# Moving the third image's first-channel products, the norm factors and the last filter chunk of a fused convolution and attention kernel

## The chip, the cores and the metric

The kernel runs on one core of a Trainium2 chip. The metric is the device time of one execution in microseconds (us). Before the change it was 2292.45 us, the median of three runs (2290.4, 2292.45, 2292.69). The engines are named as in the profile: PE is TensorE (PEld its weight loads), DVE is VectorE, ACT is ScalarE, POOL is GpSimd, SP is SyncE, which here only issues DMAs.

## The reference

Eight images of 512 channels by 32x32 pixels in fp32. `_gn` is a group norm over 32 groups, `bn_eval` a scale and shift per channel, and `cbs` a convolution, `bn_eval` and silu.

```python
def bot_attention(x, qkv_w, rw, rh):          # 4 heads of 64, 1024 pixels
    q, k, v = conv2d(x, qkv_w, 0)             # split into heads
    logits = jnp.einsum('bhdi,bhdj->bhij', q, k + (rw + rh)) * HD ** (-0.5)
    a = jax.nn.softmax(logits, axis=-1)
    return jnp.einsum('bhij,bhdj->bhdi', a, v)

t = cbs(_gn(x), cv1_w, cv1_bn, 0)             # 1x1, 512 -> 512
ys = [t[:, :256], t[:, 256:]]
for i in range(2):
    z = cbs(ys[-1], m_cv1_w[i], m_cv1_bn[i], 1)    # 3x3, 256 -> 256
    z = bot_attention(z, m_qkv_w[i], m_rw[i], m_rh[i])
    z = silu(bn_eval(conv2d(z, m_cv2_w[i], 0)))    # 1x1, 256 -> 256
    ys.append(ys[-1] + z)
out = x + cbs(concatenate(ys), cv2_w, cv2_bn, 0)   # 1x1, 1024 -> 512
```

## The kernel before, in words

**Tiling.** An image is held as 128-channel chunks of 1024 pixels. The images go in four pairs (`p` from 0 to 3, `ia` and `ib`); the change concerns the first pair and what precedes it. Line numbers are those of the kernel before, which the profile uses. Work of a later image is done ahead of its pair, where an engine has room: the first 1x1 convolution (`cv1`) of the third image's first 256 output channels (`y0`, two chunks `oc` 0 and 1) is made during the first pair's 3x3 convolution; the rest of it in the attentions.

**Group norm** (`group_norm_part`, L737 on). PE sums the channel means over groups (`gm_ps`), DVE turns them into `gm` and `dev`, PE sums `dev` (`gv_ps`), DVE adds eps (`gr`, L714), POOL takes the power (L715), DVE makes `shift` (L751), and ACT applies scale and shift in place (L757), by chunk `c` and half (512 pixels). Then PE makes the 1x1 products (L503, in `conv1x1`). It is a generator: each `next(norm)` issues one stage.

**The 3x3 convolution** (`conv3x3`) is a Winograd convolution of both images of a pair at once: the input `y1` is transformed by DVE (`tiles_in`, L525 to L580, into `v_in`), the filters by DVE and ACT (`make_u`, below), PE multiplies (L626, `c_ps`), ACT copies a part (`c_m`, L631), and DVE transforms back (L647 to L675) into `z`, which ACT passes through silu (L476). It runs in six turns: two output chunks `oc` by three rows `i` of the transform. In a turn PE makes the products `inner` (`cps` 1 and 2) and then `outer` (0). `between` is a dictionary of callbacks, called before the part `(turn, first cp)`: turn 1 to 6, first cp 1 for the inner and 0 for the outer part.

**Filters** (`make_u`, L390 to L430). A filter chunk is 128 input by 128 output channels of a 3x3 filter. It is transformed in eight steps of a generator: for rows `i` 2, 0, 1 a triple of `tensor_tensor` and a triple of `scalar_tensor_tensor` (L416 to L421, with the ACT copies L414 and L415), and a "mid" triple for row 0 (L398 to L400) and for row 1 (L402 to L404). POOL stores the result to DRAM (L427), and SP loads it later as a unit of the ring buffer `u`. The second convolution's filters (n=1) are made in the first pair: chunk (0,0) by `early` in the first qkv projection, (0,1) and (1,0) in the first attention, (1,1) after it, around `m2_a`.

**Attention** (`attention_fast`). Groups g of 0 to 3 (chunk by half) of eight key blocks, in four pairs of blocks per group. For each pair PE makes logits (L996, `l_ps`), ACT the exponentials (L1000, `pt`), DVE adds them into `acc` (L1014, L1016), PE multiplies by v (L1030, `av_ps`). At the end of a group ACT and DVE empty `av_ps` into z (L1037, L1038), PE sums `acc` over partitions (L1047, `s_ps`), DVE makes the reciprocal `rc`, which goes over DRAM (SP) and comes back spread out as `rs` for the scaling of z (L1102). `av_ps` has one PSUM buffer (`ps_av`); the logits share three (`ps_big`). `behind` is a dictionary of hooks: the key g, or (g, at) with at 1 to 3, is called after that pair of blocks. `hooks` builds it; a step of the filter generator (`step_u`) or of a norm (`step_norm`), or a single extra, may hang on each.

**What sets the order.** Each engine takes its instructions in the order that a scheduler writes down when the kernel is built. It follows the program's order and its own priorities; `tc.issue_after(ins)` adds an edge, so that what is issued inside the block comes after `ins`, if it runs on the same engine. PE orders its products of the third image after a product of the convolution in this way. DMAs stand in the queue of the engine that issues them: SP's for most loads, POOL's for stores and `late` loads.

**Around the change, in order of time:** the second image's norm (about 40 to 46 us) and products, the input transforms of both images, the third image's norm, the convolution (from 77.64) with the third image's products before its turn 3, the first qkv projection, the first attention (`l_ps` from 159.67), `m2_a` and the second projection (224.65 to 267.30), and the second attention (267.30 to about 330).

Of the kernel before, what the change touches and what calls it, by code (L numbers as in the profile page):

```python
# [61 lines left out]
def kernel(  # L62
# [134 lines left out]
    def load_m2(n):  # L197
        nc.sync.dma_start(m2_sb[:, n], m_cv2_w[n].rearrange("(k p) o -> p k o", p=P))

    def make_r(n, raw=None):  # L200
        if raw is not None:
            with tc.issue_after(s.last_exp[0].ins):
                turn_r(n, raw)
            yield
        for c in range(NM):
            for half in range(NH):
                r = act.tile([P, ROWS, F], F32, tag="t", name="r_new", bufs=4)
                tt(
                    r, rw_sb[:, n, c].unsqueeze(1).to_broadcast([P, ROWS, F]),
                    rh_sb[:, n, c, ts(half, ROWS)].unsqueeze(2).to_broadcast([P, ROWS, F]), ALU.add,  # L210
                )
                nc.gpsimd.dma_start(r_dram[n][c][:, ts(half, HALF)], r.rearrange("p h w -> p (h w)"))
                yield
# [258 lines left out]
    def stages(act, small, ps_big, ps_av, n_pt):  # L472
# [7 lines left out]

        shifted, powered, k_added = [None], [None], []
        silu_in, last_product, silued, last_exp, m2_silu = [], [None], [None], [None], [None]

# [10 lines left out]

        def conv1x1(w_of, rhs_of, nk, ks=None, ps=None, ends=None, by_half=False):

# [86 lines left out]
        def conv3x3(n, vs, u_of, z, groups=G, summed=None, after=None, between={}):  # L583
# [10 lines left out]
            for oc in range(NM):  # L594
                dst = z[:, oc].rearrange("p g x -> p (g x)").rearrange("p (t r w) -> p r t w", r=4, w=F)
                for i in range(NI):
# [15 lines left out]
                    for cps in ((1, 2), (0,)):  # L612
                        if (turn, cps[0]) in between:
                            between[turn, cps[0]](product)
                        for row in range(2):
                            for cp in cps:
                                for c in range(2):
                                    ps, bank, at = places[CPS[cp][c]]
                                    to = slots(ps, bank)[:, row, at]
                                    for k in range(NM):  # L620
# [3 lines left out]
                                        for h in range(2):  # L624
                                            o = slice(h * HD, (h + 1) * HD)
                                            product = nc.tensor.matmul(  # L626
                                                to[o], us[cp][:, k, row, c, o], rhs,
                                                start=(k == 0), stop=(k == NM - 1),
                                            )
# [108 lines left out]
        def group_norm_part(xts, by_act=0, behind=lambda c: None, spill=False):  # L738
# [12 lines left out]
            stt(shift, gm, -1.0, gr, ALU.mult, ALU.mult)  # L751
            for c in range(n):
                ahead = behind(c)
                for half in range(NH):
                    part = xts[c][:, ts(half, HALF)]
                    with tc.issue_after(ahead.ins) if ahead else nullcontext():
                        applied = nc.scalar.activation(  # L757
                            part, part, AF.Identity, scale=gr[:, c : c + 1], bias=shift[:, c : c + 1]
                        )
            yield multiplied, read, applied, powered[0]  # L760
# [446 lines left out]

        def cv1_products(w_of, xts, oc, ks=range(NX), ps=None, by_half=False):
            return conv1x1(
                lambda k: w_of(k, oc), lambda k, half: xts[k][:, ts(half, HALF)], NX, ks, ps, (0, NX - 1), by_half  # L1210
            )
# [489 lines left out]
    for p in range(NP):  # L1701
# [68 lines left out]
        if p == 0:  # L1770
            with tc.issue_after(powered.ins):
                first_taps, second_taps = [load_late(0, k, inside(Y2[k])) for k in range(NM)]
        z = new_z()
        t = s.conv3x3(
            0, vs, u_of(0), z, summed=None if direct else z[:, :, 0], after=last_out,
            between={(2, 1): third_norm, (2, 0): third_y0} if direct else {},
        )
        xs = norm = None
        if more:
            if direct:  # L1780
                xs = xs_third
            else:
                xs = [load_x(act, ia + 2, c, NX) for c in range(NX)]
# [36 lines left out]

        def hooks(norms, us=(), extra={}):
            calls = {}
            for g in range(NG):
                for at in range(4):
                    key = (g, at) if at else g
                    calls[key] = [step_norm] if key in norms else []
                    if 4 * g + at in us:
                        calls[key].append(step_u)
                    if key in extra:
# [6 lines left out]
        if p == 0:  # L1836
# [7 lines left out]
            extra[2, 2] = lambda: late_taps.append(load_late(1, 1, inside(Y2[1])))  # L1844
            extra[3, 2] = lambda: make_sq(1, q_tiles, [t[:, j] for t in q_sums for j in range(2)])
        behind = hooks(() if p == 0 else NORM_A, range(16), extra) | {NG: begin_cv1(0, Y1[0], ia + 2)}
        if p == 0:
            behind[NG + 1] = lambda: nxt.go_on()
        end = s.attention_fast(qkv, z[:, :, 0], at_of(ia, 0), behind, at_once=p == 0)
        for made in more_u:  # L1850
            pass
# [36 lines left out]
        else:  # L1888
# [52 lines left out]
        def parts_of(ocs):  # L1941
# [5 lines left out]

        behind = hooks(NORM_B, (), {}) | {
            NG + 1: begin_cv1(1, Y1[1], ia + 3)
# [254 lines left out]
```

## Time and profile before

| What | us |
|---|---|
| median of three runs | 2292.45 |
| the profiled execution, its own time | 2295.04 |
| its span, first to last instruction | 2293.5 |
| PE busy | 2223.7 |
| DVE busy | 1753.5 |
| ACT busy | 1098.3 |
| POOL busy | 205.3 |

The mean granted clock of PE is 0.991 of full speed. PE is busy in 97% of the span. A line of a timeline gives start, length, engine, line, operation, output and inputs, tile shapes, type and count, and in square brackets the idle time before it with what ended it. A line of waits gives the engine, the tile and line that waited, what it waited for, the total, the number of times, and the longest. One logical 128x512 fp32 product counts as two matmul records in the trace. A line of busy time by stage gives the stretch and its length, then for each engine the busy time and the number of instructions, then the granted clock (1.00 is full), the share of the DMA engines and GB/s.

### The profile page before, as it was taken

The numbers are of one execution on the slowest core, as the hardware profiler recorded it, in microseconds if no ns is written. First come the engines' busy times: TensorE is split into PE (matmuls) and PEld (weight loads), VectorE is DVE, ScalarE is ACT, GpSimd is POOL, SyncE is SP. The second block draws the span as 40 slices with busy tenths as digits, with TensorE's granted clock in tenths as the row PEclk, the third lists the DMA queues.
The fourth block names the chain that finished last, engine by engine and source line by source line (L and its number), as shares of the span: only waits on it lengthen the run. The fifth ranks groups of instructions, "written<-read, shape, count | busy, mean of one in ns | idle before, by whom it ended". The sixth has DMA issues, their size and how long they took to land.

```text
span 2293.5 us, 40534 instructions
## 1 busy us (share of the span) xinstructions
PE 2223.7 (97%) x16338; PEld 1083.1 (47%) x16338; DVE 1753.5 (76%) x2701; ACT 1098.3 (48%) x1361; POOL 205.3 (9%) x409
## 2 busy tenths in 40 slices
PE   7899999999999999999999999999999999999997
PEld 3563437443465443734347443654345643473443
DVE  7879789778758689886857868986784868886742
ACT  7445452555225666366323666445622455335533
POOL 2212110000120000000021000000012000000002
PEclk9999999999999999999999999999999999999999
DMA  7743626322473233612168141532137611251115
GB/s 244 276 153 117 216 76 248 106 69 71 107 224 136 75 121 96 213 46 84 52 151 266 33 164 45 169 124 75 57 79 179 215 53 42 70 196 42 48 29 134
DMA packets 128420, 281.06 MB, mean 123 GB/s; under 512 B 34112, under 2 KB 56364, under 8 KB 127200
## 3 DMA queue, kind: packets, MB, share of 16 engines
q1 hardware_dynamic: 100240, 192.25, 26.2%
q0 software_dynamic: 27984, 86.13, 12.6%
q8 instruction: 131, 2.15, 0.4%
q14 instruction: 65, 0.53, 0.1%
HBM read 210.29 MB, written 68.03 MB: 121 GB/s over the span
## 4 chain that ended last, share of the span: by engine, by line
PE 73%; DVE 20%; ACT 3%; issue 2%; DMA 1%; POOL 0%; DVEq 0%; SPq 0%; ACTq 0%; POOLq 0%
PE av_ps L1030 16%; PE l_ps L996 16%; PE c L1248 8%; PE p_ps L886 6%; PE c_new L1248 6%; PE ps L503 6%; PE m_ps L1228 4%; DVE acc L1016 2%; PE pv_ps L892 2%; PE x_ps L1348 2%; PE c_ps L626 2%; DVE c_e L650 1%; PE s_ps L1047 1%; DVE c_t L647 1%; DVE c_t L648 1%
## 5 line engine op out<-in xcount | busy, mean ns | idle before, releaser
L1000 ACT ACTIVATE pt<-l_ps 128x1024 f32<-128x1024 f32 x512 | 495.8, 1023 | 361.3 <-PE l_ps L996 329.5
L1016 DVE TENSOR_TENSOR acc<-acc,pt 128x1024 f32<-128x1024 f32 x384 | 469.9, 1224 | 97.9 <-ACT pt L1000 74.8
L1030 PE MATMUL av_ps<-pt,vT 64*64 64x512 f32 x4096 | 490.4, 596 | 12.6 <-DVE z L1038 12.3
L996 PE MATMUL l_ps<-q,kr 64*64 64x512 f32 x4096 | 488.1, 592 | 1.6 <-ACT pt L1000 0.8
L1030 PEld LDWEIGHTS av_ps<-pt,vT 64*64 64x64 f32 x4096 | 155.6, 133 | 288.3 <-issue 239.8
L996 PEld LDWEIGHTS l_ps<-q,kr 64*64 64x64 f32 x4096 | 158.9, 134 | 274.2 <-issue 253.8
L626 PEld LDWEIGHTS c_ps<-v_in,u 128*64 128x64 f32 x4320 | 235.7, 137 | 5.3 <-issue 5.3
L626 PE MATMUL c_ps<-v_in,u 128*64 128x128 f32 x4320 | 237.5, 273 | 0.0
L1228 PE MATMUL m_ps<-z,m_sb 128*128 128x512 f32 x256 | 112.5, 592 | 0.0
L886 PE MATMUL p_ps<-t_z,sq 128*128 128x512 f32 x224 | 108.0, 601 | 3.6 <-DVE c_t L648 3.6
L631 ACT COPY c_m<-c_ps 128x512 f32<-128x512 f32 x48 | 28.1, 586 | 164.7 <-PE c_ps L626 117.5
L1014 DVE TENSOR_TENSOR acc<-pt 128x1024 f32<-128x1024 f32 x64 | 78.0, 1219 | 36.2 <-ACT pt L1000 36.2
L476 ACT ACTIVATE t<-m_ps,bh,sh 128x512 f32<-128x512 f32 x64 | 46.4, 774 | 86.4 <-PE m_ps L1228 86.4
L886 PE MATMUL p_ps<-z,sq 128*128 128x512 f32 x168 | 80.8, 604 | 0.2 <-ACT m_z L923 0.2
L1298 POOL DMA_DIRECT2D c_out<-in_x_dram x56 | 50.0, 976 | 309.1 <-ACT c_out L476 306.7
L1228 PEld LDWEIGHTS m_ps<-z,m_sb 128*128 128x128 f32 x256 | 48.3, 190 | 58.8 <-issue 56.9
L476 ACT ACTIVATE z<-z,bh,sh 128x512 f32<-128x512 f32 x64 | 47.8, 806 | 27.8 <-DVE z L675 27.8
L476 ACT ACTIVATE c_out<-cz,bh,sh 128x512 f32<-128x512 f32 x14 | 16.7, 1297 | 91.4 <-DVE cz L1325 91.4
L1038 DVE TENSOR_TENSOR z<-av_ps,z 128x512 f32<-128x512 f32 x64 | 44.1, 688 | 20.6 <-ACT z L1037 20.6
L1102 DVE TENSOR_TENSOR z<-z,rs 128x512 f32<-128x512 f32 x64 | 43.9, 687 | 18.8 <-DMA rs<-r_dram 18.4
L886 PEld LDWEIGHTS p_ps<-t_z,sq 128*128 128x128 f32 x224 | 39.2, 192 | 36.1 <-issue 36.1
L647 DVE TENSOR_TENSOR c_t<-c_ps,c_m 128x512 f32<-128x512 f32 (+1 forms) x56 | 34.1, 610 | 28.7 <-ACT c_m L631 28.7
(308 smaller groups left out, 3192.5 us busy)
## 6 DMA issues: line engine op xcount, KB each, us to landing
u<-u SPq DMA_DIRECT2D x135, 512.0 KB
sq<-sq SPq DMA_DIRECT2D x42, 384.0 KB
rs<-r_dram SPq DMA_DIRECT2D x118, 128.0 KB
x<-in_x_dram SPq DMA_DIRECT2D x28, 512.0 KB
r_in<-r SPq DMA_DIRECT2D x28, 512.0 KB
y_in<-y SPq DMA_DIRECT2D x28, 512.0 KB
c_out<-in_x_dram POOLq DMA_DIRECT2D x56, 256.0 KB, 5.4
out_dram<-c_out POOLq DMA_DIRECT2D x56, 256.0 KB, 3.7
```

The lines of the kernel that those rows point to most:

```text
L476: silued[0] = nc.scalar.activation(dst, src, AF.Silu, scale=sh[:, k : k + 1], bias=bh[:, k : k + 1])
L503: last_product[0] = nc.tensor.matmul(ps[:, half, :], w_of(k), rhs_of(k, half), start=(k == begin), stop=(k == end))
L626: product = nc.tensor.matmul(to[o], us[cp][:, k, row, c, o], rhs, start=(k == 0), stop=(k == NM - 1),)
L647: tt(m[:, :, 0::2], slots(inner_ps, 0)[..., qs], m24[..., qs], ALU.add)
L886: nc.tensor.matmul(ps[:, o, :], w[:, o, :], rhs, start=not onto, stop=True, skip_group_check=onto)
L996: nc.tensor.matmul(ps[kh * HD : (kh + 1) * HD, hd, :], kr[r, c, o : o + HD], q[r, c, ts(half, HALF)], start=True, stop=True,)
L1000: last_exp[0] = exp = nc.scalar.activation(pt, ps, AF.Exp, scale=SCALE)
L1014: return nc.vector.tensor_tensor(accs[g], pt[0], pt[1], ALU.add)
L1016: ins = nc.vector.tensor_tensor(accs[g], accs[g], pt[i], ALU.add)
L1030: nc.tensor.matmul(avs[g][hd * HD : (hd + 1) * HD, kh, :], vT[r, j, o : o + HD], pt[i][r, hd, :], start=(j == 0), stop=(j == NJ - 1),)
L1228: nc.tensor.matmul(pss[half][:, oc, :], m2_sb[:, n, k, ts(oc, P)], ao[:, k, ts(half, HALF)], start=(k == 0), stop=(k == NM - 1),)
L1248: nc.tensor.matmul(ps[:, o, :], w[:, k, ts(o, P)], rhs[part][:, c], start=(k == 0 and not onto), stop=(k == KB - 1), skip_group_check=onto,)
```

## The change

Five things change.

1. **Factors ahead of filter steps** (second image's norm). `behind_u` issues three filter steps between the norm's activations; they now come after the norm's addition of eps (`added_eps`, L714) on DVE.
2. **The third image's `y0` products at three places.** Its norm ends in turn 1 (key (1,0)) instead of turn 2, and the third row of the input transforms becomes a step of its own, at (2,1). Chunk 0 (both halves) is made at (2,0), the first half of chunk 1 at (3,1), and its second half after the convolution, ahead of the qkv projection. `conv1x1` and `cv1_products` take `halves`. The silu of a chunk (the eviction of its PSUM tile) comes after its last half. With `spill` the norm's activations are sorted, all first halves ahead of all second halves.
3. **The norm factor ahead of the eviction.** Since the third norm stands at (1,0), its `gr` stands on DVE ahead of the eviction of turn 1's products (L647 on). `conv_product` holds the convolution's latest product.
4. **The DMAs of `make_sq`** are issued on POOL after those of r (`put_r`).
5. **The last filter chunk** (1,1) moves from around `m2_a` into the second attention, one step on each of the hooks 0, 1, 4, 6, 7, 8, 11 and 12 (4g + at). In the first attention the steps hang on hooks 0 to 11 only, and what is left is issued after it. Of the units of the second convolution three are loaded ahead instead of six.

```diff
 def make_r(n, raw=None):
...
-                nc.gpsimd.dma_start(r_dram[n][c][:, ts(half, HALF)], r.rearrange("p h w -> p (h w)"))
+                put_r[0] = nc.gpsimd.dma_start(r_dram[n][c][:, ts(half, HALF)], r.rearrange("p h w -> p (h w)"))
...
 def conv1x1(...):
-            order = [(k, half) for k in ks for half in range(NH)]
+            order = [(k, half) for k in ks for half in halves]
...
 def conv3x3(...):
                         if (turn, cps[0]) in between:
-                            between[turn, cps[0]](product)
+                            between[turn, cps[0]](conv_product[0])
...
 def gn_rstd(...):
-            read = nc.vector.tensor_scalar(gr, ps, GN_EPS, None, ALU.add)
+            added_eps[0] = read = nc.vector.tensor_scalar(gr, ps, GN_EPS, None, ALU.add)
...
 def group_norm_part(...):
-            for c in range(n):
-                ahead = behind(c)
-                for half in range(NH):
-                    part = xts[c][:, ts(half, HALF)]
-                    with tc.issue_after(ahead.ins) if ahead else nullcontext():
-                        applied = nc.scalar.activation(
-                            part, part, AF.Identity, scale=gr[:, c : c + 1], bias=shift[:, c : c + 1]
-                        )
+            parts = [(c, half) for c in range(n) for half in range(NH)]
+            for c, half in sorted(parts, key=lambda a: a[1]) if spill else parts:
+                ahead = behind(c) if half == 0 else ahead
+                part = xts[c][:, ts(half, HALF)]
+                with tc.issue_after(ahead.ins) if ahead else nullcontext():
+                    applied = nc.scalar.activation(
+                        part, part, AF.Identity, scale=gr[:, c : c + 1], bias=shift[:, c : c + 1]
+                    )
...
     def behind_u(c):
         if c == 2:
-            for _ in range(3):
-                next(chunk)
+            with tc.issue_after(s.added_eps[0].ins):
+                for _ in range(3):
+                    next(chunk)
         return copied_u[0] if c else None
...
-    def third_y0(done):
-        y0s = new_y0()
-        for oc in Y0S:
-            ps = ps_av.tile([P, NH, HALF], F32, tag="av", name="ps")
+    third_y0s, third_ps = [], {}
+
+    def third_y0(oc, halves=range(NH)):
+        def run(done):
+            if not third_y0s:
+                third_y0s.extend(new_y0())
+            if oc not in third_ps:
+                third_ps[oc] = ps_av.tile([P, NH, HALF], F32, tag="av", name="ps")
             with tc.issue_after(done.ins):
-                s.cv1_products(w1_of, xs_third, oc, ps=ps, by_half=True)
-            s.cv1(w1_of, xs_third, y0s, None, [oc], {oc: (ps, NX)})
-        keep_y0(G, y0s)
+                s.cv1_products(w1_of, xs_third, oc, ps=third_ps[oc], by_half=True, halves=halves)
+            if NH - 1 in halves:
+                s.cv1(w1_of, xs_third, third_y0s, None, [oc], {oc: (third_ps[oc], NX)})
+
+        return run
...
     def third_norm(done):
         with tc.issue_after(last.ins), tc.issue_after(s.silued[0].ins), tc.issue_after(done.ins):
             next(norm)
+
+    def third_parts(done):
         for g in range(G):
             s.tiles_in(Y1[g], putter(vs, g), [2], ecs[g])
...
+        in_first = {
+            (1, 0): third_norm, (2, 1): third_parts, (2, 0): third_y0(0), (3, 1): third_y0(1, [0]),
+        }
...
-            between={(2, 1): third_norm, (2, 0): third_y0} if direct else {},
+            between=in_first if direct else {},
...
             if direct:
                 xs = xs_third
+                third_y0(1, [1])(s.conv_product[0])
+                keep_y0(G, third_y0s)
...
-            extra[3, 2] = lambda: make_sq(1, q_tiles, [t[:, j] for t in q_sums for j in range(2)])
-        behind = hooks(() if p == 0 else NORM_A, range(16), extra) | {NG: begin_cv1(0, Y1[0], ia + 2)}
+            def with_sq():
+                with tc.issue_after(put_r[0].ins):
+                    make_sq(1, q_tiles, [t[:, j] for t in q_sums for j in range(2)])
+
+            extra[3, 2] = with_sq
+        behind = hooks(() if p == 0 else NORM_A, {i: 1 for i in range(12)}, extra) | {NG: begin_cv1(0, Y1[0], ia + 2)}
...
-        for made in more_u:
+        while step_u():
             pass
...
             if direct:
-                more_u = filters([(1, 1, late_taps[0])])
-                with tc.issue_after(end.scaled.ins):
-                    for _ in range(5):
-                        made = step_u()
-                last = m2_a()
+                m2_a()
                 end.check()
...
-                with tc.issue_after(made.ins), tc.issue_after(last.ins):
-                    for made in more_u:
-                        pass
-                feed(units(1)[:6])
+                feed(units(1)[:3])
...
-        behind = hooks(NORM_B, (), {}) | {
+        if direct:
+            more_u = filters([(1, 1, late_taps[0])])
+        behind = hooks(NORM_B, {i: 1 for i in (0, 1, 4, 6, 7, 8, 11, 12)}) | {
             NG + 1: begin_cv1(1, Y1[1], ia + 3)
         }
...
         end = s.attention_fast(qkv, z[:, :, 1], at_of(ib, 0), behind, at_once=True)
+        while step_u():
+            pass
```

More of the change, by code (lines that the diff above doesn't have):

```diff
@@ L198, in load_m2 @@
         nc.sync.dma_start(m2_sb[:, n], m_cv2_w[n].rearrange("(k p) o -> p k o", p=P))
+    put_r = [None]
     def make_r(n, raw=None):
@@ L479, in silu @@
             return silued[0]
-        shifted, powered, k_added = [None], [None], []
-        silu_in, last_product, silued, last_exp, m2_silu = [], [None], [None], [None], [None]
+        shifted, powered, added_eps, k_added = [None], [None], [None], []
+        silu_in, last_product, silued, last_exp, m2_silu, conv_product = [], [None], [None], [None], [None], [None]
         def exp_table():
@@ L493, in big, with conv1x1 @@
             return ps_big.tile([P, 2, HALF], F32, tag="big", name="p_ps")
-        def conv1x1(w_of, rhs_of, nk, ks=None, ps=None, ends=None, by_half=False):
+        def conv1x1(w_of, rhs_of, nk, ks=None, ps=None, ends=None, by_half=False, halves=range(NH)):
             if ps is None:
@@ L625, in conv3x3 @@
                                             o = slice(h * HD, (h + 1) * HD)
-                                            product = nc.tensor.matmul(
+                                            conv_product[0] = nc.tensor.matmul(
                                                 to[o], us[cp][:, k, row, c, o], rhs,
@@ L1206, in attention_general, with cv1_products @@
             return ao
-        def cv1_products(w_of, xts, oc, ks=range(NX), ps=None, by_half=False):
+        def cv1_products(w_of, xts, oc, ks=range(NX), ps=None, by_half=False, halves=range(NH)):
             return conv1x1(
-                lambda k: w_of(k, oc), lambda k, half: xts[k][:, ts(half, HALF)], NX, ks, ps, (0, NX - 1), by_half
+                lambda k: w_of(k, oc), lambda k, half: xts[k][:, ts(half, HALF)], NX, ks, ps, (0, NX - 1), by_half,
+                halves,
             )
@@ L1819, in begin_cv1, with hooks @@
             return run
-        def hooks(norms, us=(), extra={}):
+        def hooks(norms, us={}, extra={}):
             calls = {}
@@ L1826, in hooks @@
                     calls[key] = [step_norm] if key in norms else []
[L1827 to L1828 removed]
+                    calls[key] += [step_u] * us.get(4 * g + at, 0)
                     if key in extra:
```

## The prediction

> **What bounds the kernel now.** I read the page first (busy time by engine), then TensorE's waits from 30 to 335 us (the stretch that the diff touches), its timeline, VectorE's waits and timeline in that stretch, and busy time by stage. All times are of the profiled execution.
>
> The page puts TensorE at 97% of the span, so only its stalls, and stretches at a lower clock, can be won.
>
> ```profile
> PE 2223.7 (97%) x16338; PEld 1083.1 (47%) x16338; DVE 1753.5 (76%) x2701; ACT 1098.3 (48%) x1361; POOL 205.3 (9%) x409
> ```
>
> TensorE's waits, 30 to 335 us (total, times, longest):
>
> ```profile
> PE av_ps L1030 <- DVE z L1038: 5.6, 4, 3.1
> PE ps L503 <- DVE c_t L648: 4.1, 1, 4.1
> PE c_ps L626 <- DVE v_in L579: 3.3, 1, 3.3
> PE ps L503 <- ACT x_second L757: 2.6, 1, 2.6
> PE ps L503 <- ACT y_half L476: 2.4, 1, 2.4
> PE s_ps L1047 <- DVE acc L1016: 1.5, 1, 1.5
> ```
>
> Some 20 us. Where they lie is in its timeline (start, length, count, idle before):
>
> ```profile
> 46.43 0.70 PE L503 MATMUL ps<-x_second,w_cols 128*128 128x512 f32 x1 [2.58 <-ACT x_second L757]
> ...
> 77.64 7.13 PE L626 MATMUL c_ps<-v_in,u_new 128*64 128x128 f32 x96 [3.26 <-DVE v_in L579]
> ...
> 101.83 8.83 PE L503 MATMUL ps<-x,w_cols 128*128 128x512 f32 x16 [2.36 <-ACT y_half L476]
> 110.59 5.46 PE L626 MATMUL c_ps<-v_in,u_new 128*64 128x128 f32 x96
> 115.88 15.89 PE L626 MATMUL c_ps<-v_in,u 128*64 128x128 f32 x288
> 131.70 1.98 PE L503 MATMUL ps<-z,w_qkv 128*128 128x512 f32 x4
> 137.74 8.23 PE L503 MATMUL ps<-z,w_qkv 128*128 128x512 f32 x12 [4.06 <-DVE c_t L648]
> ```
>
> The third image's products (about 90 to 110) stand ahead of the convolution's third turn at 110.59. VectorE, which finishes every turn, runs dry behind them (its waits, 30 to 160):
>
> ```profile
> DVE c_t L647 <- ACT c_m L631: 9.0, 3, 5.1
> DVE kr L843 <- PE ps L503: 4.3, 2, 3.7
> DVE taps L402 <- ACT u_new L415: 2.0, 1, 2.0
> ```
>
> and then ends late, so TensorE waits 4.06 us for z at 137.74. By stage (stretch, length, then busy PE, PEld, DVE, ACT, POOL; clock):
>
> ```profile
> 225.00:267.00 42.00, 42.00 (x120) 21.02 (x118) 35.41 (x68) 14.38 (x21) 11.04 (x22) 1.00 0.79 268
> 267.00:330.00 63.00, 60.51 (x553) 21.67 (x552) 46.87 (x59) 41.80 (x50) 5.51 (x9) 0.97 0.25 81
> ```
>
> Between the attentions TensorE never stops; in the second attention it already stops for VectorE.
>
> [...] after the waits of 3.26, 2.36, 4.06 and 3.10 us the granted clock reads 0.50 for 3.4 or 6.8 us; after 2.58 us[...], not at all. [...] the tiny gr (L714) runs at 43.79, after L402 and L403, though its product began at 41.65 and VectorE was idle from 40.74 to 42.72. [...] Here u_new stores land in 2.7 us (median, 160 to 335).
>
> **The change part by part.**
>
> *Second image's norm.* The factor gr now precedes the filter steps that waited for a ScalarE copy: it can run at 42.0, shift at 43.6 (POOL's power keeps its 1.21), x_second from 43.8 instead of 45.56, and the 2.58 us stall falls to 0.8. But TensorE's next stall, 3.26 us at 77.64, ends with VectorE's v_in; an earlier TensorE only waits longer there. Only what VectorE's chain gains counts. The 1.97 us idle is partly filled, five filter steps (2.44 us) go behind shift, interleaving recovers about 1 us: −0.5 to +0.5 net, I take −0.4. A stall near 5 us can bring a longer half clock at 77 us; from 77 to 90 VectorE limits the turns, which hides it.
>
> *Third image.* 16 products of two records each (32 records at 0.43 us: 27.73/64). They ran in one piece apart from four; now 8 logical products stand inside turn 2, four inside turn 3, and four after the convolution. The norm's end moves to turn 1, with gr right behind v_in, ahead of c_t; ScalarE writes all first halves first: x from 86.9 instead of 89.69. The order now on TensorE: first-channel products 90 to 97, y_half 97 to 99.2, one half of the second channel's products 99.3 to 102.8, turn 3 from about 103.5 instead of 110.59. Without the pile VectorE's waits of 5.14, 3.47, 0.41 and 0.32 us for c_m go: z's second channel, first image, ends at 137.26−9.3 = 127.9, and I allow 0.5 for hand-overs: 128.4. TensorE ends the convolution at 103.5+5.46+15.89+0.5 = 125.4 and fills the gap to 128.9 with the last four products (8×0.43). Then four qkv records (1.98) on z's first channel to 130.7; z's second channel is through ScalarE by 130.0 (two silus of 0.8). Twelve more at full clock, 5.2, end at 135.9. Before they ended at 137.74+8.23 = 145.97: **−10.1**. Bounds: if turn 3 starts 2 us later or some c_m waits stay, −7; if the chain of the first part adds, −11. What is late next is VectorE's own chain of turns.
>
> *qkv_raw to POOL after r.* These DMAs held POOL's queue from 114 to 133 without anyone waiting. Behind the r stores: 0.
>
> *First attention.* Steps come at 12 hooks, the last four after it; 0.42 us triples lie a little earlier, so z of the third group comes 0.7 later. The 3.1 us stall stays, its half clock (16 records 3.69 instead of 1.90, next 16 3.07: 3.0 lost) may fall differently[...]. +0.7−0.7 = 0; bounds −1.5 to +1.5.
>
> *Last filter chunk.* Eight steps, 24 VectorE instructions: 18 of 0.42 in six triples (1.25 each), six of 0.55 (two mids, 1.77): 11.0 us. Leaving 238.7 to 255.1 gives nothing: TensorE is 42.00 of 42.00 us busy there. In the second attention VectorE has gaps (waits there: 6.4, 5.8 and 3.3 us, 15.5), but not evenly. The steps hang on hooks 0, 1, 4, 6, 7, 8, 11, 12 (four to a group). The first two fall in a loose group. Five more, about 7.0 us, come ahead of the third group's z, where VectorE has only 0.20+1.79+0.60+1.01 = 3.6 of idle left, and from 303.82 to 319.9 none:
>
> ```profile
> 315.11 1.22 DVE L1014 TENSOR_TENSOR acc<-pt 128x1024 f32<-128x1024 f32 x1
> 316.24 0.69 DVE L1038 TENSOR_TENSOR z<-av_ps,z 128x512 f32<-128x512 f32 x1
> ```
>
> So z moves from 316.24 to about 319.6; TensorE already waits for it (1.48 at s_ps, 1.01 at av_ps), so +3.4 passes on whole. Half clock now holds 318 to 321.4; a longer stall adds about 0.6: **+4.0**. Bounds: 0, if gaps take all; +10.4, all 7.0 exposed and a full half-clock window (3.4) more. The last step is followed by 2.6 us of idle at 320: free.
>
> *SP's queue.* The loads of the chunk's units wait for its stores (last triple 324.5, POOL 325.2, +2.7: 328); behind them in the queue stand the rc store and rs loads of the third group. They land at 334 to 335; scaling needs them by about 335, with 0.6 slack ahead of m_ps at 336.97. +0.3, bounds 0 to 1.
>
> Sum: −0.4−10.1+0+4.0+0.3 = −6.2. Span 2293.5 to 2287.3; the profiled run itself took 2295.04, 2.6 over the median 2292.45, so against the median: **2286.3**. What this measurement tells from no change is about 0.2%, 4.6 us: faster means below 2287.9.
>
> **Rivals.**
> - *Second attention absorbs* (0.20): gaps of 15.5 us exceed 11.0. Against it: the gap-free stretch before 316.24. −10.5+0.5: 2282.5.
> - *Conv gain given back* (0.17): the same mechanism as in the forecast, 8 to 9 us exposed, since the ScalarE copies of three of the steps (0.40+0.39 each) also stand ahead of exps: −10.5+9: 2291.
> - *Does not do what it says* (0.05): the second channel's four products inside turn 3 wait on the single PSUM buffer that y_half must empty, and hold turn 3 as before; the gaps stay, −3.5+4: about 2292.5.
> - *Slower* (0.12): the chunk costs more in the second attention than the convolution saves. Place: acc and z of groups two and three, on VectorE; price 11.0 exposed in full, two half-clock windows (3.4 lost), rs late by 1: +15.4, against −10.5: 2297.4. It decides beyond 10.5 exposed, and shows beyond 15. Against it: exps leave VectorE idle 2.61 us at 320 and 1.57 at 282, which some steps must find.
>
> **How the numbers follow.** The forecast, 2286.3, has 0.46, its own range 2283.5 to 2287.9. Faster: 0.46+0.20 = 0.66. Same: 0.17+0.05 = 0.22. Slower 0.12. The range, 2280 to 2293, holds the first three cases and the fourth; it leaves out the slower case and tails of 0.06.
>
> **What would show it.** In the trace after: no wait for c_t before qkv and none of VectorE for c_m beyond 1 us; first l_ps near 149.2 (159.67 before); second attention (first l_ps to the s_ps that ends it, 267.30 to 329.03, 61.7 us) at about 65.8; DVE z of its third group 3 us later against its start; 225 to 267's counterpart as long as before. Wrong if the second attention grows by under 1 or over 8 us, if turn 3 starts later than 106, or if a stall appears after 330 (rs late).

## The result and the profile after

The changed kernel took 2286.45 us, median of 11 runs (2282.5 to 2290.58); the kernel before, 2292.34, median of 11. The ratio is 0.9974, with a 95% interval of 0.9965 to 0.9983: 0.26% faster. The profiled execution of the kernel after took 2286.45 us with a span of 2284.6, against 2295.04 and 2293.5 before.

TensorE's waits from 30 to 330 us, kernel after (line numbers are two to three higher than before):

```profile
PE av_ps L1032 <- DVE z L1040: 8.2, 5, 3.1
PE c_ps L628 <- DVE v_in L581: 5.0, 2, 4.8
PE s_ps L1049 <- DVE acc L1018: 2.1, 1, 2.1
PE ps L505 <- ACT x_second L759: 0.6, 1, 0.6
PE ps L505 <- ACT y_half L478: 0.5, 1, 0.5
```

The wait for c_t ahead of qkv (4.1 us) is gone, the one for y_half has shrunk from 2.4 to 0.5, that for x_second from 2.6 to 0.6. The longest one for v_in grew from 3.3 to 4.8, and those for z and acc, in the attentions, from 7.1 to 10.3. VectorE, which waited 9.0 us for c_m before, no longer waits for it at all; from 75 to 147 us it has one line of waits left:

```profile
DVE kr L845 <- PE ps L505: 2.4, 2, 1.5
```

TensorE's timeline in the convolution:

```profile
76.47 5.75 PE L628 MATMUL c_ps<-v_in,u_new 128*64 128x128 f32 x64 [4.77 <-DVE v_in L581]
...
87.75 7.13 PE L505 MATMUL ps<-x,w_cols 128*128 128x512 f32 x16
94.82 1.97 PE L628 MATMUL c_ps<-v_in,u_new 128*64 128x128 f32 x32
97.29 3.70 PE L505 MATMUL ps<-x,w_cols 128*128 128x512 f32 x8 [0.50 <-ACT y_half L478]
101.18 5.46 PE L628 MATMUL c_ps<-v_in,u_new 128*64 128x128 f32 x96 [0.19 <-DVE v_in L581]
106.47 15.89 PE L628 MATMUL c_ps<-v_in,u 128*64 128x128 f32 x288
122.29 3.70 PE L505 MATMUL ps<-x,w_cols 128*128 128x512 f32 x8
125.83 7.03 PE L505 MATMUL ps<-z,w_qkv 128*128 128x512 f32 x16
```

The three places are to be seen (16, 8 and 8 records at L505), and TensorE waits for nothing from turn 3 (101.18) to the end of qkv. In the second attention it is the other way round (start, length):

```profile
303.46 0.64 PE L1049 MATMUL s_ps<-acc,ones 128*32 128x256 f32 x8 [2.12 <-DVE acc L1018]
306.36 3.42 PE L1032 MATMUL av_ps<-pt,vT 64*64 64x512 f32 x16 [2.26 <-DVE z L1040]
...
331.02 2.84 PE L1231 MATMUL m_ps<-z,m_sb 128*128 128x512 f32 x6 [0.45 <-DVE z L1104]
```

The same stall, at the end of the third group, was 1.48 and 1.01 us before, and m_ps had none. A smaller one is new at the second group's z (0.47 us). Marks of the two traces, from TensorE's timeline (start in us), with e1 and e2 of the experiments below:

| Mark | before | after | difference | e1 | e2 |
|---|---|---|---|---|---|
| first c_ps | 77.64 | 76.47 | −1.17 | 78.10 | 77.43 |
| first l_ps, first attention | 159.67 | 146.56 | −13.11 | 148.19 | 159.69 |
| first l_ps, second attention | 267.30 | 253.84 | −13.46 | 255.30 | 267.33 |
| s_ps at its end (L1064 before, L1066 after) | 329.03 | 318.19 | −10.84 | 315.71 | 332.55 |
| n=1 convolution | 364.53 | 354.39 | −10.14 | 351.21 | 368.04 |
| from there to the end of the span | 1928.97 | 1930.21 | +1.24 | 1927.19 | 1929.66 |

So the convolution brought 11.9 us (82.03 from first c_ps to first l_ps became 70.09), the second attention took 2.6 back, and the scaling behind it 0.7.

### The profile page after: what moved, and what is told of

The parts are those of the page before. It is cut to its first block, busy times and chain, and to the rows that moved or that the text cites. A ratio compares the mean times of both kernels' runs of the same rounds, so it can differ in the third digit from the quotient of the medians.

```text
span 2284.6 us, 40531 instructions
## 1 busy us (share of the span) xinstructions
PE 2218.8 (97%) x16338; PEld 1081.3 (47%) x16338; DVE 1753.0 (77%) x2701; ACT 1097.9 (48%) x1361; POOL 204.7 (9%) x409
## 4 chain that ended last, share of the span: by engine, by line
## 5 line engine op out<-in xcount | busy, mean ns | idle before, releaser
L1351 PE MATMUL x_ps<-t_x,sw 128*128 128x512 f32 x128 | 55.9, 592 | 0.0
```

The costliest lines, as they stand in the source:

```text
L1351: nc.tensor.matmul(ps[:, o, :], w[:, c, ts(o, P)], rhs[c], start=(c == 0 and not onto), stop=(c == 1), skip_group_check=onto,)
```

## The experiments

Each ran beside the kernel before; the time is a median, the ratio is to the kernel before as it ran beside it. Medians of different experiments are compared by their ratios. 11 us are 0.48%. No run undid the norm factor ahead of the eviction (item 3 of the change), the sorting of the norm's activations by halves (in item 2) or the order of `make_sq`'s DMAs (item 4) alone, so their shares are not known. Outside the traces of before and after, half clock is read from the length of records. In the kernel before, 16 records of av_ps that elsewhere took 1.95 us behind a wait, and the 16 of l_ps after them, 1.90 us elsewhere, took 3.19 and 2.41 behind the waits of 1.48 and 1.01 us; there the granted clock reads 0.50 from 317.5 to 321.0.

**e1: the last filter chunk back.**

```diff
-        if direct:
-            more_u = filters([(1, 1, late_taps[0])])
-        behind = hooks(NORM_B, {i: 1 for i in (0, 1, 4, 6, 7, 8, 11, 12)}) | {
+        behind = hooks(NORM_B, {}, {}) | {
...
+                more_u = filters([(1, 1, late_taps[0])])
+                with tc.issue_after(end.scaled.ins):
+                    for _ in range(5):
+                        made = step_u()
...
-                feed(units(1)[:3])
+                feed(units(1)[:6])
```

> The kernel after, with the last filter chunk put back around m2_a (and six units loaded ahead), nothing else undone. My theory: the chunk costs in the second attention because VectorE is already late there, and cost nothing around m2_a. First l_ps to the s_ps that ends the second attention falls from 64.4 us (after) back to 61.7, the 0.45 us stall ahead of m_ps goes, the conv of n=1 starts 3.3 us earlier (about 351), and the time is about 2283. Rival (the attention absorbs the chunk, the 2.6 us are where half-clock windows happen to fall): second attention stays near 64, time 2286. Rival (the chunk around m2_a delays that stretch now that it starts earlier): 225 to 267's counterpart longer than 42.7 us, time 2286 or more.

Measured: 2280.33 us, ratio 0.9956 (0.9943 to 0.9969). Waits of TensorE in the second attention and just behind it, e1:

```profile
PE s_ps L1049 <- DVE acc L1018: 1.9, 1, 1.9
PE av_ps L1032 <- DVE z L1040: 1.0, 1, 1.0
```

and in the same stretch of the kernel after:

```profile
PE av_ps L1032 <- DVE z L1040: 2.7, 2, 2.3
PE s_ps L1049 <- DVE acc L1018: 2.1, 1, 2.1
PE m_ps L1231 <- DVE z L1104: 0.4, 1, 0.4
```

The attention fell from 64.35 to 60.41 us. That is 1.3 less than the 61.73 of before, though its waits are 0.4 longer, because no half clock followed: the records behind them took 1.95 and 1.90 us, not 3.19 and 2.41. The stretch ahead of it, where the chunk now stands again, is as long as in the other two (35.59 us from its s_ps to l_ps): there the chunk costs nothing. The n=1 convolution starts 3.2 us earlier than after, as expected; the time is lower by a little more than that (0.18% by the ratios, 4.1 us).

**e2: only the chunk moved**, on the kernel before (the reverse of e1's edit).

> The kernel before, with only the last filter chunk moved into the second attention. My theory: second attention 61.7 to about 64.5 to 65.5, m_ps stalls by about half a us, 3.3 us longer in all: 2295.6. Rival (absorbed): 2292.3, attention 61.7. Rival (more than I said): attention over 68, 2300.

Measured: 2295.76 us, ratio 1.0024 (1.0016 to 1.0031). The attention took 65.22 us instead of 61.73; the n=1 convolution came 3.5 us later. This part of the change alone makes the kernel slower.

**e3: only the second image's norm.** The kernel before, with one edit:

```diff
-            for _ in range(3):
-                next(chunk)
+            with tc.issue_after(s.added_eps[0].ins):
+                for _ in range(3):
+                    next(chunk)
```

> The kernel before, with only the filter steps of the second image's norm put behind its factor. My theory: x_second's stall falls from 2.6 to 0.6, but the wait for v_in grows from 3.3 to 4.8; the convolution starts 1.2 us earlier at most (76.5), and as VectorE carries on from there the first l_ps comes 0.4 to 1.2 earlier: 2291.5. Rival (TensorE's stall is what counts): 2 us, 2290.3, with the v_in wait unchanged. Rival (nothing): 2292.3.

Measured: 2293.73 us, ratio 1.001 (1.0003 to 1.0016). TensorE's waits, e3, 30 to 340 us:

```profile
PE c_ps L626 <- DVE v_in L579: 4.9, 1, 4.9
PE ps L503 <- DVE c_t L648: 4.1, 1, 4.1
...
PE ps L503 <- ACT x_second L757: 0.6, 1, 0.6
```

The 2 us won at x_second are lost at v_in, as both I and the trace of the kernel after had it. The trace is 0.7 us ahead at the n=1 convolution; the time is 0.1% behind, and the interval just excludes no change. Nothing in the trace shows a stage that loses by the edit, so this 0.1% stays unexplained; in e12 the sign is the other way.

**e5b: the third image's products in one pile.** The kernel after, with

```diff
-            (1, 0): third_norm, (2, 1): third_parts, (2, 0): third_y0(0), (3, 1): third_y0(1, [0]),
+            (1, 0): third_norm, (2, 1): third_parts, (2, 0): both_y0,
...
-                third_y0(1, [1])(s.conv_product[0])
```

where `both_y0` makes both chunks whole.

> The kernel after, with all 16 of the third image's products again in one place, ahead of the outer part of turn 2; its norm stays early. My theory (what counts is that the pile kept turn 3, and so VectorE, waiting): y_half wait of 2.4 back, turn 3 starts near 107 to 109 instead of 101.2, VectorE waits for c_m about 5 us, qkv waits for c_t about 4 and pays a half-clock window; first l_ps 154 to 157 instead of 146.6; time about 2295. Rival (the earlier norm alone made the gain): l_ps within 2 us of 146.6, time 2286 to 2288.

Measured: 2293.73 us, ratio 1.0009 (1.0003 to 1.0016): the whole gain is gone. TensorE's timeline, e5b:

```profile
97.45 7.13 PE L505 MATMUL ps<-x,w_cols 128*128 128x512 f32 x16 [0.71 <-ACT y_half L478]
104.51 5.78 PE L628 MATMUL c_ps<-v_in,u_new 128*64 128x128 f32 x101
...
132.94 8.13 PE L505 MATMUL ps<-z,w_qkv 128*128 128x512 f32 x12 [4.07 <-DVE c_t L650]
```

The wait for c_t is back in full (4.07) and the half clock behind it (8.13 us for 12 records, while 16 take 7.03 in the kernel after; in before it was 8.23, with the granted clock at 0.50 from 136.6 to 143.5). From first c_ps to first l_ps: before 82.03, e5b 77.73, after 70.09. Of the 11.9 us the three places bring 7.6, and everything else in the convolution, above all the earlier norm and its first halves, 4.3. VectorE waits again, 3.5 us for c_m and 1.9 for c_ps (I had about 5). TensorE's wait for y_half was only 0.71, not the 2.4 that I expected: here the outer products of turn 2 stand between the two chunks and cover most of the eviction. And turn 3 could start at 104.5, only 3.3 later than after; that is enough, with those waits, for VectorE to end late.

**e8: the second chunk wholly behind the convolution.** The kernel after, with

```diff
-            ... (2, 0): third_y0(0), (3, 1): third_y0(1, [0]),
+            ... (2, 0): third_y0(0),
...
-                third_y0(1, [1])(s.conv_product[0])
+                third_y0(1)(s.conv_product[0])
```

> The kernel after, with both halves of the third image's second channel chunk behind the convolution, and none inside turn 3. My theory: in after the half inside turn 3 fills time in which TensorE would wait for v_in of the third row (turn 3 starts right when v_in is there, 101.2); so turn 3 starts no earlier, TensorE stops there for 3 to 4 us, and the eight records come on top behind the convolution: from the first c_ps to the first l_ps 70.1 becomes 73.6, perhaps 1.7 more for a half-clock window; 2290 to 2291.5. Rival (VectorE's turns are the bound from turn 2 on, TensorE has slack there): 70 to 71, 2286.5.

Measured: 2292.66 us, ratio 1.0003 (0.9995 to 1.0011). TensorE's timeline, e8:

```profile
94.76 1.97 PE L628 MATMUL c_ps<-v_in,u_new 128*64 128x128 f32 x32
101.66 8.27 PE L628 MATMUL c_ps<-v_in,u_new 128*64 128x128 f32 x96 [4.93 <-DVE v_in L581]
...
125.58 7.13 PE L505 MATMUL ps<-x,w_cols 128*128 128x512 f32 x16
```

Turn 3 starts no earlier (24.8 us behind the first c_ps, 24.7 in the kernel after); TensorE waits 4.93 us for v_in and then pays 2.8 at half clock (8.27 for 96 records instead of 5.46), and the second half stands behind. First c_ps to first l_ps: 76.42 us, 6.3 over after: 3.5 for the products and 2.8 of half clock. I had 3.5 and up to 1.7; half clock cost 1.1 more than that. The half inside turn 3 is a filling for a hole that would be there anyway.

**e7: the chunk at other hooks.** The kernel after, with

```diff
-        behind = hooks(NORM_B, {i: 1 for i in (0, 1, 4, 6, 7, 8, 11, 12)}) | {
+        behind = hooks(NORM_B, {i: 1 for i in (0, 1, 2, 3, 12, 13, 14, 15)}) | {
```

> The kernel after, with the same eight steps of the last filter chunk in the second attention, but on hooks 0 to 3 and 12 to 15 (first and last group) instead of 0, 1, 4, 6, 7, 8, 11, 12. My theory (the cost is the place: steps ahead of the third group's z on a VectorE without gaps): waits for acc and z of the third group fall from 4.4 us (after) to 2.9 or less, as with the chunk back (e1); up to 1 us more at the first group's z; attention 62 to 63 instead of 64.4; and as the loads of the chunk's units now stand behind those of rs in SP's queue, the 5.3 us wait of the scaling for rs goes. Time 2282 to 2284. Rival (the amount counts, not the place): attention 64 or more, time 2286.

Measured: 2285.38 us, ratio 0.9972 (0.9961 to 0.9982). TensorE's waits in the second attention, e7:

```profile
PE av_ps L1032 <- DVE z L1040: 2.3, 2, 1.3
PE s_ps L1049 <- DVE acc L1018: 1.5, 1, 1.5
PE s_ps L1066 <- DVE acc L1018: 0.3, 1, 0.3
```

The third group's waits are those of before again (1.48 and 1.01), so the place does count. But 1.33 came up at the first group's z, where I had said up to 1, and half clock fell behind the third group's stall (16 records of av_ps took 2.88 us and 16 of l_ps 2.72, in e1 1.95 and 1.90): the attention took 63.84 us, between what the two theories said (62 to 63, and 64 or more). So my theory holds for the third group's stall and not for the price: the first group had no room for four steps. The time (2282 to 2284 expected, 2286 by the rival) tells neither from the other, nor this kernel from the kernel after (0.9974). The scaling's wait for rs is gone, and m_ps does not stall.

That last point shows the queue. This is SP's timeline in the kernel after (start, length, instruction). The four unit loads take 8.06 us, most of it waiting for POOL's stores of u_new (6.4 us of waits in SP's own list). The write of rc goes out behind them, and the loads of rs wait 5.1 us for it to land and go out at 321.04:

```profile
307.37 8.06 SPq L301 DMA_DIRECT2D u<-u  x4
315.53 0.37 SPq L1094 DMA_DIRECT2D r_dram<-rc  x1
321.04 1.10 SPq L1096 DMA_DIRECT2D rs<-r_dram  x2
```

In e7 those two stand ahead of the unit loads, and SP waits only 1.1 us for the write of rc:

```profile
315.73 0.33 SPq L1094 DMA_DIRECT2D r_dram<-rc  x1
317.14 1.10 SPq L1096 DMA_DIRECT2D rs<-r_dram  x2
...
320.30 6.53 SPq L301 DMA_DIRECT2D u<-u  x3
```

**e9: another load taken out of the second attention.** The kernel after, with the third row of Y2's input transforms ahead of it, in the first pair only:

```diff
                 tiles_later(1, None)
+                if direct:
+                    tiles_later(2, None)
...
-        behind[2, 1] = lambda: (apply(), tiles_later(2))
+        behind[2, 1] = apply if direct else lambda: (apply(), tiles_later(2))
```

> The kernel after, with the third row of the input transforms of Y2 (some 9 us of VectorE in one piece, at hook (2,1) of the second attention) made ahead of that attention, in the first pair only; the filter chunk stays in the attention. My theory (what the second attention pays for is VectorE's load ahead of the third group's z): the waits for acc and z of 4.4 us go, attention 64.4 to about 60, the stretch ahead stays at 42.6 since TensorE has no wait there; time 2281. Rival (the waits are set by ScalarE's exps or the PSUM buffer): attention stays over 63; rival (the stretch ahead is delayed): 42.6 grows by 3 or more.

Measured: 2285.06 us, ratio 0.9967 (0.9955 to 0.9979). TensorE's waits from the second attention on, e9:

```profile
PE m_ps L1231 <- DVE z L1104: 2.3, 2, 1.2
PE av_ps L1032 <- DVE z L1040: 0.8, 2, 0.5
```

The attention took 58.73 us (about 60 expected) and the stretch ahead of it, from s_ps to l_ps, 35.59 us, as in the kernel after. The waits for z and acc fell from 4.8 us to 0.8, with the chunk still in the attention: they are VectorE's load, not ScalarE's exps or PSUM. But the loads of rs went out at 317.96 only, behind the unit loads, and with the attention 5.6 us shorter m_ps had to wait 2.3 us for the scaling. The n=1 convolution starts 3.8 us earlier than after. The time is 1.4 lower, which the two intervals don't tell apart; in this trace the later stretches, which are the same program, ran 2.3 us longer than in after's.

**e10: the first attention.** e1, with

```diff
-            extra = {key: lambda: next(r_steps) for key in ((0, 3), (1, 1), (1, 3), (2, 1), (2, 3))}
+            extra = {key: lambda: next(r_steps) for key in ((0, 3), (2, 1), (2, 3), 3, (3, 1))}
...
-        behind = hooks(() if p == 0 else NORM_A, {i: 1 for i in range(12)}, extra) | ...
+        behind = hooks(() if p == 0 else NORM_A, {i: 1 for i in (0, 1, 2, 3, 5, 7, 8, 9, 10, 11, 12, 13, 14, 15)}, extra) | ...
```

> The kernel with the chunk back (e1), and in the first attention the two r additions of the second group moved to the fourth, two of its filter steps and two others later (steps on hooks 0-3, 5, 7-15 instead of 0-11). Theory: its 3.1 us wait for z of the second group is VectorE's load there, as in the second attention: the wait falls below 1 us, the half-clock window behind it goes (up to 1.7), later groups wait up to 2 us more; first attention (first l_ps to the s_ps that ends it, 71.5 us with e1) 67 to 69; time about 2277. Rival (load only moves on): 71 to 72, 2280.

Measured: 2277.72 us, ratio 0.9933 (0.992 to 0.9947). The first attention took 66.89 us instead of 71.52; its waits are one line, with 5.5, 3, 3.1 in e1:

```profile
PE av_ps L1032 <- DVE z L1040: 2.3, 3, 1.2
```

That is 3.2 us of waits; the rest is mostly the half clock behind e1's stall of 3.1 us (16 records of av_ps in 3.46 us), which e10 does not have (1.95, behind a wait of 0.71). The same load spread later is cheaper here. This is the fastest kernel of the study, with e12.

**e11: e9 and e10 together, with SP's queue in order.** The chunk on hooks 0, 1, 4, 6, 8, 10, 13 and 14.

> First attention as in e10, and the third row of Y2's transforms ahead of the second attention as in e9; the filter chunk in the second attention, its last steps on hooks 13 and 14 (0, 1, 4, 6, 8, 10, 13, 14), so that SP's queue has the loads of rs ahead of the unit loads. Theory: in e9 the gain of the second attention was lost again at the scaling, where rs came late behind the unit loads; with the queue in this order the waits of 2.3 us ahead of m_ps go, and from the second attention's first l_ps to the n=1 convolution it takes 94 to 95.5 us (e9 97.0, e10 97.2, after 100.6). Time 2275. Rival (rs is late for another cause, or the last filter steps now delay the last group): 97 or more, 2278.

Measured: 2281.13 us, ratio 0.9956 (0.9941 to 0.997). The mechanism came as expected: TensorE doesn't wait in the second attention or at m_ps, and from its first l_ps to the n=1 convolution it takes 93.41 us (after 100.55). But it was paid for ahead of it; TensorE's only wait from 212 to 332 us in e11 is

```profile
PE p_ps L858 <- ACT ypad L478: 4.8, 1, 4.8
```

a product of the second projection that waits for ScalarE's silu to empty its PSUM tile, which none of the other kernels has. The waits of ScalarE and VectorE from 205 to 262 us lead back from it:

```profile
ACT ypad L478 <- DVE ypad L1239: 7.7, 1, 7.7
DVE st L690 <- DMA x<-in_x_dram: 13.5, 1, 13.5
```

The silu waited for VectorE's `ypad`. This stood on VectorE behind the statistics (`st`) of the next image's x, and these waited 13.5 us for the loads of x (2.4 in the kernel after). In SP's queue those loads stood behind two loads of w that took 6.28 us instead of 1.11; they went out 15.2 us after the first attention's s_ps (229.78) instead of 5.1 us after it (223.36). So this is again a queue, read from the trace and not tried by a run. The stretch from that s_ps to the second attention's first l_ps took 42.75 us instead of 35.59: the wait, and the 32 records behind it, which took 9.27 us instead of 7.07 in the kernel after. That ate the gain.

**e12: e10 without the norm edit** (e3's edit undone).

> e10 with one thing undone: the filter steps of the second image's norm stand ahead of its factor, as in the kernel before. Theory: the norm edit hardly matters (VectorE's chain, not TensorE's stall, sets the start of the convolution): x_second's wait back at 2.5 us, v_in's down to about 3.3, first c_ps within 1 us of e10 and first l_ps from c_ps unchanged at 70.1; time 2277.5 to 2279. Rival (it is worth its stall of 2 us): 2279.7 or more. Rival (it costs, as the time of e3 has it): 2276 or less.

Measured: 2277.08 us, ratio 0.9945 (0.9932 to 0.9957), against 0.9933 (0.992 to 0.9947) for e10: by the ratios 0.12% slower, which the intervals don't tell from nothing. x_second's wait came back (3.1 us). First c_ps is at 77.46 here and at 78.59 in e10; from there to the first l_ps it takes 70.07 and 70.08. The edit alone was 0.1% slower in e3, and undoing it is 0.12% slower here; the two signs disagree, and neither trace has a stage that gains by it. So no worth of the second image's norm edit is shown; within about 0.1% it may go either way.

## Why the prediction was right

The time, 2286.3 against 2286.45, was right, and the mechanisms too, but for a part of the last; the sizes less so. That the two figures agree to 0.2 us is luck. By terms of the sum, up to the n=1 convolution:

| Step | predicted | traces | shown by |
|---|---|---|---|
| second image's norm | −0.4 | −1.2 | e3, e12: no worth shown |
| third image | −10.1 | −11.9 | e5b, e8 |
| first attention | 0 | −0.35 | traces only |
| chunk in the second attention | +4.0 | +2.6 | e1 +3.9, e2 +3.5 |
| rs behind SP's queue | +0.3 | +0.7 | e7 |
| sum | −6.2 | −10.1 | |

*Norm.* The step was sound: TensorE's stall moved to v_in. The start of the convolution differs by up to 2.5 us between kernels whose edits lie behind it (76.23 in e9, 78.73 in e7), so the −1.2 is not shown to be an effect of the edit. The longer half clock at 77 us came: the granted clock read 0.50 for 6.8 us (73.9 to 80.7) around the end of the wait of 4.77, and for 3.4 in before. From 77 to 90 VectorE was busy 12.5 of 13.0 us in before.

*Third image.* Mis-sized by 1.8. I placed turn 3 at 103.5, 25.9 us behind the first c_ps; it began at 101.2, 24.7 behind it, because the eight products of the first chunk (87.75 to 94.8) came about a microsecond earlier in the convolution than I had them (90 to 97). The other 0.7 us is mostly the 0.5 that I allowed TensorE behind turn 3 and that it didn't need: convolution to 122.3, then the last four products and qkv without a wait.

*First attention.* Its 3.1 us stall stayed (3.11). z of the third group came later, as I supposed: TensorE's wait for it grew from 1.12 to 1.94 us. That was offset by the half clock at the second group's stall, which cost 1.8 us (16 records of av_ps in 3.22 and 16 of l_ps in 2.38, instead of 1.90) and not 3.0: the granted clock read 0.50 for 3.4 us (183.1 to 186.5) in after, for 6.8 (194.7 to 201.5) in before, with stalls of 3.11 and 3.10. Why it was half as long is not shown; my 0.7 for it was an estimate that no trace backed.

*Chunk.* Right in place and sign. The third group's z came 2.8 us later against the attention's start (51.8 us instead of 48.9), not 3.4, and the stall there grew from 2.5 to 4.4 us; the second group's stall of 0.47 I had not foreseen. The trace of e2 gave 3.5, that of e1 against after 3.9 (64.35−60.41). In both pairs TensorE's waits grew by 2.0 to 2.4 us; much of the rest is half clock, which cost nothing in e1's attention, 1.5 us in after's (16 records of av_ps in 3.42 instead of 1.90), 1.8 in before's (3.19 and 2.41 for twice 16) and 2.4 in e2's (3.69 and 2.53). So the 0.6 that I added for a longer stall, an estimate, is what e2 shows against before; in after half clock cost less. VectorE's waits for ScalarE there fell from 15.5 us (6.4, 5.8 and 3.3) to 8.1 (4.0, 2.2 and 1.9), so 7.4 of the 11.0 us found a gap; I had taken the gaps ahead of the third group's z for 3.6. (In both traces 1.76 us of these waits lie just behind the attention's last s_ps; and the half clock that I had from 318 to 321.4 stands at 317.5 to 321.0. Neither changes the sum. My upper bound of +10.4 does not add up as written: 3.4 us at half clock lose 1.7 us, not 3.4, as the rival's sum below it has it, so that bound is 8.7.)

*SP's queue.* Right in the place, and in the small price: VectorE waits 5.3 us for rs, and that costs TensorE 0.45. The last store went out about where I had put it (310.9, which is 324.4 with the 13.5 us that the attention started earlier; I had 325.2). But the larger cause was another. rc was made by 314.4, and SP had finished the unit loads at 315.4, so the queue held it for 1.1 us only. The write of rc then took 5.1 us, behind the unit loads, against 1.1 in e1 and e7, where no unit load stands ahead of it; that I had not counted. One of my signs of being wrong, a stall after 330, did appear (m_ps, 0.45 us); my own sum had 0.3 for it, so I had set that sign too sharply.

*The median.* The traces' early part gives −10.1, the spans −8.9, the medians −5.9. Of the 4.2 us between the first and the last, 1.2 are later stretches that happened to run longer in the trace after, 2.7 are that before's profiled execution was that much over its median (2295.04 against 2292.34), while after's was at it, and 0.3 that a span and its execution's time differ. My sum was too small by 3.9 against the traces, and these hid it. In all eleven traces of changed kernels the gain at the n=1 convolution, taken against the one trace of before, is larger than the gain by the ratios, by 0.8 to 6.4 us (3.0 on average). So a part of the −10.1 may be that trace of before, and the change is worth the 5.9 us of the medians. Where in before's execution the 2.7 us lie, the traces don't show. Where such differences can come from is told in the last section.

The rivals: "absorbs" falls with e2 (+0.24%, the attention 3.5 us longer); "slower" falls with the result, since no pair of traces has the chunk cost more than 3.9 us, where it needed over 10.5; "does not do what it says" falls with turn 3 at 101.2; "given back" does not reach the 8 to 9 us that it wanted.

## What to carry to other kernels

Filler work belongs where the engine that it fills would wait anyhow: half of the third image's second chunk is free at turn 3 (e8 shows what happens without it) and late at turn 2 (e5b). A piece of work on a second engine is free while the first one never waits there (the chunk around m2_a, 35.59 us with it in e1 and without it in the kernel after), as long as it doesn't make a load late that the stage needs (e11); it is dear in a stage that already waits for that engine (3.5 us in e2, 3.9 by e1); before moving it, look at whose stalls the target stage has. When a moved step issues DMAs, look at what stands behind its waiting loads in the queue; here the scaling's loads did (VectorE waited 5.3 us for rs).

## What the runs showed of the hardware

From the n=1 convolution on, all twelve kernels are the same program. Cut at the starts and ends of the attentions into 28 stretches, 18 agree to 0.03 us over all twelve traces. The others differ, the last one by 2.4 us, and three attentions by 1.7 us, in steps: the attention that starts at 825 us (clock of before) and the stretch behind it together took about 145.7, 147 or 148.6. The same stall stands in it: in e1

```profile
860.00 0.64 PE L1049 MATMUL s_ps<-acc,ones 128*32 128x256 f32 x8 [1.41 <-DVE acc L1018]
861.65 1.95 PE L1032 MATMUL av_ps<-pt,vT 64*64 64x512 f32 x16 [1.01 <-DVE z L1040]
```

and in the kernel after

```profile
863.48 0.64 PE L1049 MATMUL s_ps<-acc,ones 128*32 128x256 f32 x8 [1.42 <-DVE acc L1018]
865.12 3.13 PE L1032 MATMUL av_ps<-pt,vT 64*64 64x512 f32 x16 [1.00 <-DVE z L1040]
```

Waits equal to 0.01 us, and once the next 16 records take 1.95, once 3.13; the mean granted clock over the three microseconds around the second of these lines (861 to 864, and 865 to 868) is 1.00 in e1 and 0.63 in the kernel after. Behind this stall the 16 records took 3.13 to 3.49 us in four of the twelve traces (the kernel after, e2, e5b and e9) and 1.95 in the other eight, with the same two waits to 0.01 us.

The length of a wait does not tell by itself whether half clock follows. In the kernel before, the wait of 2.36 us for y_half had 3.4 us of it behind it (102.5 to 105.9), the 2.58 us for x_second at 46.43 none. Nor does it tell for how long: the granted clock read 0.50 for 6.8 us at the stall of 3.10 in before and for 3.4 at the one of 3.11 in after. What decides, these traces don't show.

A stall of about 2.4 us thus cost 1.8 us more here (3.13 and, for the 16 records of l_ps behind them, 2.48 in the kernel after; 1.95 and 1.90 in e1), or nothing. Between the n=1 convolution and TensorE's idle end the twelve traces have one to three such half-clock stretches (one in e1, two in the kernel before, three in the kernel after, with 1927.19, 1928.97 and 1930.21 us); all five of before and after lasted 3.4 us, which loses 1.7. By that, two of them more or fewer would make, as an estimate, 3.4 of the 8 us by which the runs of one kernel differ (2282.5 to 2290.58). For a change worth 5 us, one trace's span is not enough: compare stage by stage.
